# Where the residual stream is turned: the out projection's transposes and joins moved to the second stage's loads

## The chip, the cores and the metric

The kernel runs on one core of a Trainium2 chip. The metric is the device time of one launch in microseconds. It is 2405.47 us before the change (median of three runs, 2402.76 to 2409.40). One more execution was recorded by the hardware profiler; its own time is 2406.19 us.

## What is computed

The input x is 64 blocks of 64 channels by 1024 columns, which the kernel sees as 32 tiles of 128 tokens by H = 1024. Cut to what matters:

```python
x = x + attn(cond(x, itok_B_0_15, cond_weights), qkvw, qkvb, ow, ob)   # 32 heads of 32, softmax over 64
# second stage, cond2:
base   = x @ W.T
logits = x @ Wr.T + 5.0 * one_hot(language)        # 8 experts, the best 2, softmax of the two
lora   = sum over experts of ((x @ A_e.T) * gate_e) @ B_e
z      = base + 2.0 * lora
# feed-forward on z as bf16, each token scaled to 8 bits:
g, u   = quant(z * inv_gate) @ w_gate.T, quant(z * inv_up) @ w_up.T    # 512 wide
inter  = clip(silu(g) * u, -10, 10)
x      = x + quant(inter * inv_inter) @ w_down.T
```

`x` after the attention is called x1 here. It is needed twice: token by token, as the residual to which the last product is added, and turned (columns on the partitions, tokens along the free dimension), as the operand of the router and of `base`.

## The kernel before

The 32 tiles are taken in 16 pairs of 256 tokens. The attention works on blocks of 512 tokens and leaves its result, already turned, in DRAM. Then come two stages that run over the 16 pairs.

**The out projection** (`OutProjection`) multiplies a pair by `ow` with seven products (`Winograd`, in the order 1, 6, 7, 5, 2, 4, 3), each of 8 TensorE instructions of 128x512 in f32. Pairs 0 and 1 are woven into the end of the attention, pairs 2 to 15 run in the first loop of `second_stage`. Each product has a `rest` that adds into the tile x, which holds the input and the bias; after product 4 the first tile of the pair is complete, after product 3 the second. Each complete tile is then turned for the second stage (`turn`): 16-bit words are what a transposing DMA moves, so ScalarE copies each half of 512 columns into two planes, of low and of high halves of the words (`xh`), SP issues a transposing DMA from SBUF to SBUF (`xhT`), and some products later (`turned`) ScalarE joins the planes again into f32 words (`xTo`), which SP stores to `xT_d` in DRAM. The untouched tile is stored to the output, where the residual is kept. A pair takes four such turns.

**The second stage** is a software pipeline written out by hand: the loop body at the end of `second_stage` lists the steps of pairs p, p-1 and p-2, and each engine runs its own instructions in that order. For pair p, `load_x1` brings the pair's turned x1 in one DMA of 1 MB, a pair ahead; `router` multiplies it by the experts' matrices; `token_sums` makes the four sums that the seven products need, on VectorE; `route` chooses the experts on VectorE, with two small exponentials on ScalarE; `gates_transposed` turns the gates on TensorE (`ghp`) and ScalarE copies them to SBUF (`gT`); `lora` adds a product with gT to four of the seven products. What follows (`quant_a`, `quant_b`, `gate_or_up`, `glu`, `down`, `result`) belongs to the feed-forward. `quant_b` turns bf16 values by a transposing DMA issued by SP.

SP issues nearly all DMAs, in program order; one that has to wait for its data or its buffer holds up those behind it. Every DMA that SP issues also waits for the DMA that SP issued eight places before it, since eight semaphores are used in turn. Behind the out projection SP issues pair 1's load, and then the feed-forward's weights and rows of factors (`ig`, `iu`, `wg`, `wu`, `sg_w`, `su_w`, `ii`, `wd`, `sd_w`), 5.25 MB.

The last pair is done without the seven products (`undivided`), and its residual is read from the output (`x1_l`, `x1_ll`) and added by VectorE or GpSimd; the other pairs add by an accumulating DMA that GpSimd issues.

Of the kernel before, what the change touches and what calls it, by code (L numbers as in the profile page):

```python
# [11 lines left out]
F32 = mybir.dt.float32  # L12
# [8 lines left out]
P = 128  # L21
# [14 lines left out]
@with_exitstack  # L36
def adaln_attn_ffn(ctx: ExitStack, tc: tile.TileContext, a, out: bass.AP):
    nc = tc.nc
    x = a["x"]
    NB, C, H = x.shape  # L40
    NTOK = NB * C
    KC = H // P
    NT = NTOK // P
    BLK = 512
    PB = BLK // P
    NBLK = NTOK // BLK
    NCH = HEADS * HD // P
    HPC = P // HD

    x_t = x.rearrange("(i b) c t -> i (b c) t", b=2)  # L50
    out_t = out.rearrange("(i b) c t -> i (b c) t", b=2)

    const = ctx.enter_context(tc.tile_pool(name="const", bufs=1))
    dram = ctx.enter_context(tc.tile_pool(name="dram", bufs=1, space=bass.MemoryType.DRAM))

    ident = const.tile([P, P], F32, tag="ident", name="ident")
    make_identity(nc, ident)


    ctx_d = [  # L60
        dram.tile([P, NCH, 2 * P], F32, tag=f"ctx_d{p}", name=f"ctx_d{p}") for p in range(NT // 2)
    ]


    xT_d = [dram.tile([P, 2, KC, P], F32, tag=f"xT_d{p}", name=f"xT_d{p}") for p in range(NT // 2)]


    I = a["w_gate_t"].shape[1]
    srcs = {"wg": (a["w_gate_t"], KC, I), "wu": (a["w_up_t"], KC, I), "wd": (a["w_down_t"], I // P, H)}
    half = {  # L70
        nm: dram.tile([P, k, n], BF16, tag=nm + "_d", name=nm + "_d") for nm, (_, k, n) in srcs.items()
    }

    comb = {
        nm: dram.tile([P, 4, KC // 2, H // 2], F32, tag=nm + "_c", name=nm + "_c") for nm in ("wo", "wt")
    }
    any_i = const.tile([1, 1], I32, tag="any_i", name="any_i")
    with tc.manual_schedule(), ExitStack() as psum, ExitStack() as early:
        ps_g = psum.enter_context(tc.tile_pool(name="ps_g", bufs=4, space=PSUM, reuse_waits="tile"))
        st = early.enter_context(tc.tile_pool(name="halve", bufs=2))  # L80
        chores = halve_weights(tc, st, const, dram, srcs, half, any_i)
        chores = itertools.chain(chores, combine_quarters(tc, st, (("wo", a["ow"]), ("wt", a["w_t"])), comb))
        op = OutProjection(tc, a, x_t, out_t, ctx_d, xT_d, ps_g, comb, KC, H)
        attention(tc, a, x_t, ctx_d, ident, dram, ps_g, KC, PB, NBLK, NCH, HPC, H, C, chores, early, op)
        second_stage(tc, a, out_t, xT_d, ident, ps_g, KC, NT, H, C, half, comb, op)

    inexact = nc.values_load(any_i[0:1, 0:1], min_val=0, max_val=1)
    with tc.If(inexact != 0):
        feed_forward(tc, a, x_t, out_t, ctx_d, ident, KC, NT, PB, H, C, None)
# [1053 lines left out]
    B.update(T1=t1, T2=t2, T3=t3, T4=t4)  # L1143


def token_quarters(raw, KQ):
    return {f"B{h + 1}{t + 1}": raw[:, t, h * KQ:(h + 1) * KQ, :] for h in range(2) for t in range(2)}


def load_quarters(tc, pool, comb, nm, src, KQ, HH):  # L1150

    v = quarters(src)
# [14 lines left out]
class OutProjection:  # L1167

    def __init__(self, tc, a, x_t, out_t, ctx_d, xT_d, ps_g, comb, KC, H):
        self.tc, self.a, self.x_t, self.out_t, self.ctx_d, self.ps_g, self.comb = tc, a, x_t, out_t, ctx_d, ps_g, comb
        self.xT_d, self.turning = xT_d, []
        self.KC, self.H = KC, H
        self.NPAIR = len(ctx_d)
        self.stack = ExitStack()
        self.st = {}
# [38 lines left out]
        T = self.tp.tile([P, 4, KQ, P], F32, tag="T", name=f"To_{p}")  # L1216
        sums_of_tokens(self.tc.nc.vector, T, s["B"])

    def turn(self, p, t):

        nc, n = self.tc.nc, self.H // 2
        for f in range(2):
            h = self.hp.tile([P, 2, n], I16, tag="h", name=f"xh_{p}_{t}_{f}")
            nc.scalar.copy(h, planes(self.st[p]["x"][:, t, f * n:(f + 1) * n]))  # L1224
            hT = self.hp.tile([P, 2, n], I16, tag="hT", name=f"xhT_{p}_{t}_{f}")
            nc.sync.dma_start(
                hT.rearrange("p h (k q) -> p (h k) q", q=P), h.rearrange("p h n -> p (h n)"), transpose=True
            )
            self.turning.append((p, t, f, hT))

    def turned(self):
        nc, n, KQ = self.tc.nc, self.H // 2, self.KC // 2
        for p, t, f, hT in self.turning:
            xT = self.hp.tile([P, KQ, P], F32, tag="xT", name=f"xTo_{p}_{t}_{f}")
            nc.scalar.copy(planes(xT.rearrange("p k q -> p (k q)")), hT)  # L1235
            nc.sync.dma_start(self.xT_d[p][:, t, f * KQ:(f + 1) * KQ, :], xT)
        self.turning = []

    def pair(self, p):

# [4 lines left out]
        def one(i):  # L1245
# [8 lines left out]
            def rest():  # L1254
                x, ps = self.st[p]["x"], u.pop(("ps", i))
                if i in (6, 3):
                    self.turned()
                if i in (1, 6, 7):
                    u[i] = self.up.tile([P, HH], F32, tag=f"u{i}", name=f"ou{i}_{p}")
                    if i == 1:  # L1260
# [9 lines left out]
                if i == 5 and p + 1 < self.NPAIR:  # L1270
                    self.prepare(p + 1)
                if i in (4, 3):
                    self.turn(p, t)
                if i == 3:
                    for t in range(2):
                        nc.sync.dma_start(self.out_t[2 * p + t], x[:, t, :])
# [6 lines left out]
        return [one(i) for i in Winograd.ORDER]  # L1283


def second_stage(tc, a, out_t, xT_d, ident, ps_g, KC, NT, H, C, half, comb, op):


    nc = tc.nc
# [9 lines left out]
    with ExitStack() as ctx:  # L1299
# [2 lines left out]
        AT, loads_t = load_quarters(tc, wa, comb, "wt", a["w_t"], KQ, HH)  # L1302
        loads_t = iter(loads_t)
        ws = ctx.enter_context(tc.tile_pool(name="ws3", bufs=1, reuse_waits="tile", side="right"))
        xp1 = ctx.enter_context(tc.tile_pool(name="x3", bufs=2, reuse_waits="tile", side="right"))

        def load_row(name, src, n, pool=None):
            t = (pool or w).tile([P, n], F32, tag=name, name=name)
# [2 lines left out]

        st1 = {}

        def load_x1(p):
            s = st1[p] = {}
            s["xT"] = xp1.tile([P, 2, KC, P], F32, tag="x", name=f"x1T_{p}")
            nc.sync.dma_start(s["xT"], xT_d[p])

        awr = ws.tile([P, KC, ER + E], F32, tag="awr", name="awr")
        lang_i = ws.tile([P, NT], I32, tag="lang_i", name="lang_i")  # L1320
        bm = ws.tile([P, H], F32, tag="bm", name="bm")

        def first_loads():
            load_x1(0)
            nc.sync.dma_start(awr[:, :, 0:ER], a["a_t"].rearrange("(k p) n -> p k n", p=P))
            nc.sync.dma_start(awr[:, :, ER:ER + E], a["wr_t"].rearrange("(k p) n -> p k n", p=P))
            for r in range(2):
                nc.sync.dma_start(lang_i[r * C:(r + 1) * C, :], bcast_rows(a["lang"][r], C))
            nc.sync.dma_start(bm, a["b_t"].rearrange("e r o -> (e r) o"))


        for p in range(2, NPAIR):
# [5 lines left out]
                ld()  # L1338
            if p == NPAIR - 3:
                first_loads()  # L1340
        op.turned()
        op.stack.close()


# [3 lines left out]
        sm = ctx.enter_context(tc.tile_pool(name="sm3", bufs=2, reuse_waits="tile"))  # L1348

        st = st1  # L1350
        load_x1(1)
        ig = load_row("ig", a["inv_gate"], H)
        iu = load_row("iu", a["inv_up"], H)
        wt_b = {}
# [31 lines left out]

        def token_sums(p):
            s = st[p]
            s["B"] = token_quarters(s["xT"], KQ)
            T = p1p.tile([P, 4, KQ, P], F32, tag="T", name=f"T_{p}")  # L1390
            sums_of_tokens(nc.vector, T, s["B"])

        def router(p):
            s = st[p]
            pr = ps_h.tile([P, 2, ER + E], F32, tag="h", name=f"pr_{p}")
            for t in range(2):
                for k in range(KC):
                    nc.tensor.matmul(  # L1398
                        pr[:, t, :], s["xT"][:, t, k, :], awr[:, k, :],
                        start=(k == 0), stop=(k == KC - 1), skip_group_check=True,  # L1400
                    )
            s["pr"] = pr
# [76 lines left out]
        def undivided(p, t, n):  # L1479
# [5 lines left out]
            for h in range(2):  # L1485
                for k in range(KQ):
                    nc.tensor.matmul(
                        ps, s["xT"][:, t, h * KQ + k, :], AT[f"A{n + 1}{h + 1}"][:, k, :],
                        start=(h == 0 and k == 0), stop=(h == 1 and k == KQ - 1), skip_group_check=True,
                    )  # L1490

# [131 lines left out]
        def result(p, t, *adds):  # L1623
# [3 lines left out]
            for n in range(2):  # L1627
# [1 line left out]
                    y[:, hs[n]], s.pop(("pd", t, n)), si, sd_w[:, hs[n]], ALU.mult, ALU.mult  # L1629
                )  # L1630
                if adds:
                    adds[n % len(adds)].tensor_add(y[:, hs[n]], y[:, hs[n]], s["x", t][:, hs[n]])
                    nc.sync.dma_start(out_t[2 * p + t, :, hs[n]], y[:, hs[n]])
            if not adds:

# [8 lines left out]
        for p in range(NPAIR - 1):  # L1644
            q, r = p - 1, p - 2
            old, last = q >= 0, r >= 0
            do(p > 0, load_x1, p + 1)
            do(old, after, q, 3)
            do(last, scaled, r, 1, "u")
            do(last, glu, r, 1)  # L1650
# [9 lines left out]
            route(p)  # L1660
            after(p, 6)
            do(old, quant_b, q, 0, "u")
            base(p, 7)
            if p == NPAIR - 2:

# [18 lines left out]
            do(old, quant_b, q, 1, "u")  # L1684
            do(old, quant_a, q, 0, "i")
            base(p, 4)
            after(p, 4)
            do(old, gate_or_up, q, 1, "g")
            quant_a(p, 0, "g", (q, 0, "i") if old else None)
# [7 lines left out]


        p, q, r = NPAIR - 1, NPAIR - 2, NPAIR - 3
        st[q]["x", 1] = p1p.tile([P, H], F32, tag="xl", name="x1_l")  # L1700
        nc.sync.dma_start(st[q]["x", 1], out_t[2 * q + 1])
        xl = xp1.tile([P, 2, KC, P], F32, tag="x", name="x1_ll").rearrange("p t k n -> p t (k n)")
        for t in range(2):
            st[p]["x", t] = xl[:, t, :]
            nc.sync.dma_start(xl[:, t, :], out_t[2 * p + t])
        after(q, 3)
        scaled(r, 1, "u")
        glu(r, 1)
# [14 lines left out]
        quant_a(q, 1, "u", (q, 1, "g"))  # L1723
        completed(p, 0, 0)
        completed(p, 0, 1)
        rounded(p, 0, 0)
        rounded(p, 0, 1)
        result(r, 1)
# [104 lines left out]
```

## Time and profile before

| What | us |
|---|---|
| Median of three runs | 2405.47 |
| The profiled execution, its time | 2406.19 |
| The profiled execution, its span (first to last instruction) | 2404.4 |
| TensorE busy in the span | 2367.6 |
| VectorE, ScalarE, GpSimd busy | 1334.5, 936.2, 418.7 |
| Out projection, pairs 2 to 15 (1375 to 1712) | 24.0 a pair |
| Second stage, from 1712; a steady pair | 41.75 |

Times inside the profile are microseconds from the start of the span. In a timeline a line gives the start, the length, the engine, the line of the kernel, the operation with its output and inputs, how many instructions were merged, and in brackets how long the engine had been idle and what ended that. SPq is the instruction queue of SP, which issues DMAs: its length is the issue, not the transfer. A "transpose" on SP is a transposing DMA; a COPY of 128x1024 int16 on ScalarE is either a parting into planes (`xh<-xo`) or a join (`xTo<-xhT`).

The groups of the page that carry the turning, with busy time, mean of one in ns, and the idle time of the engine before them:

```profile
L1224 ACT COPY xh<-xo 128x1024 int16<-128x1024 int16 x64 | 64.4, 1041 | 142.8 <-DVE xo L1269 142.8
L1235 ACT COPY xTo<-xhT 128x1024 int16<-128x1024 int16 x64 | 84.7, 1337 | 58.4 <-DMA xhT<-xh 53.3
```

### The profile page before, as it was taken

Reading aid. Unit: us, or ns where it says so; the run is one execution under the profiler, and the core shown is the slowest. Engines: PE = TensorE matmul, PEld = TensorE weight load, DVE = VectorE, ACT = ScalarE, POOL = GpSimd, SP = SyncE. Lnnn points to the kernel's source line nnn. Section 1 sums busy time; section 2 is a strip of 40 time slices with the busy share of each in tenths; the row PEclk is TensorE's granted clock in tenths of the full one; section 3 lists DMA queues with packets and bytes.
Section 4 is the critical chain, followed back from the end, with each engine's and each line's share of the span. In section 5 each row is a group of like instructions: output and inputs, shape, how many; then the busy total and the mean of one; then the engine's idle time right before and its main releaser. Section 6 shows DMA issues by size and latency. Waiting matters only on the chain.

```text
span 2404.4 us, 41907 instructions
## 1 busy us (share of the span) xinstructions
PE 2367.6 (98%) x17066; PEld 1628.5 (68%) x17104; DVE 1334.5 (56%) x2584; ACT 936.2 (39%) x1220; POOL 418.7 (17%) x470
## 2 busy tenths in 40 slices
PE   8999999999999999999999999999999999999997
PEld 7888888888888888888888444444454545454452
DVE  3573474464543644633535533324377878777787
ACT  1344344343344443443434544343333333333333
POOL 4121112111122223220000333334100000000000
PEclk9999999999999999999999999999999999999999
DMA  7899799899899998997967788877733443444353
GB/s 229 217 240 248 190 228 241 221 232 220 208 232 274 212 255 230 242 237 179 207 188 196 213 257 258 275 218 248 239 77 75 90 79 83 84 86 82 70 119 76
DMA packets 612395, 453.84 MB, mean 189 GB/s; under 512 B 362465, under 2 KB 524258, under 8 KB 606690
## 3 DMA queue, kind: packets, MB, share of 16 engines
q1 hardware_dynamic: 581522, 393.91, 63.2%
q0 software_dynamic: 12240, 40.38, 7.9%
q10 hardware_dynamic: 18432, 16.79, 3.1%
q8 instruction: 137, 2.24, 0.4%
q14 instruction: 64, 0.52, 0.1%
HBM read 274.02 MB, written 91.23 MB: 152 GB/s over the span
## 4 chain that ended last, share of the span: by engine, by line
PE 92%; DMA 2%; DVE 1%; SPq 1%; issue 1%; ACT 0%; ACTq 0%; DVEq 0%
PE poa L1129 5%; PE poc L1129 5%; PE pod L1129 5%; PE psvc L530 4%; PE psva L530 4%; PE psvd L530 4%; PE pbc L1129 4%; PE pbd L1129 4%; PE pba L1129 4%; PE pskc L509 4%; PE pskd L509 4%; PE pska L509 4%; PE psqa L509 4%; PE psqd L509 4%; PE psqc L509 4%; PE pr L1398 2%
## 5 line engine op out<-in xcount | busy, mean ns | idle before, releaser
L582 ACT ACTIVATE prob<-prob 128x512 f32<-128x512 f32 x128 | 80.6, 629 | 346.7 <-DVE prob L578 338.6
L608 ACT COPY pT<-phT 128x1024 int16<-128x1024 int16 x128 | 165.4, 1339 | 25.4 <-DMA phT<-ph 21.4
L596 ACT COPY ph<-prob 128x1024 int16<-128x1024 int16 x128 | 133.5, 1043 | 63.1 <-DVE prob L590 38.4
L442 POOL COPY yB<-yhT 128x512 int16<-128x512 int16 (+1 forms) x84 | 75.8, 955 | 426.4 <-DMA yhT<-yh 426.4
L1636 POOL DMA_DIRECT2D out_dram<-y x29 | 25.2, 869 | 656.2 <-DVE y L1628 644.4
L577 DVE TENSOR_REDUCE mx<-s 128x8 f32<-128x512 f32 x128 | 87.4, 682 | 71.6 <-PE s L568 71.6
L1250 POOL TENSOR_TENSOR xo<-xo,ob 128x1024 f32<-128x1024 f32 x32 | 83.5, 2629 | 228.2 <-DVE prob L578 189.5
L509 PE MATMUL psqa<-yB,wq 128*128 128x256 f32 x512 | 121.1, 379 | 0.5 <-ACT psqp L479 0.5
L509 PE MATMUL pska<-yB,wk 128*128 128x256 f32 x512 | 120.9, 379 | 0.0
L1224 ACT COPY xh<-xo 128x1024 int16<-128x1024 int16 x64 | 64.4, 1041 | 142.8 <-DVE xo L1269 142.8
L530 PE MATMUL psva<-wv,yB 128*128 128x256 f32 x512 | 115.8, 379 | 0.0
L1129 PE MATMUL poa<-woA,cx 128*128 128x512 f32 x256 | 115.3, 593 | 0.0
L1129 PE MATMUL pba<-wtA,x1T 128*128 128x512 f32 x240 | 107.9, 592 | 0.0
L1235 ACT COPY xTo<-xhT 128x1024 int16<-128x1024 int16 x64 | 84.7, 1337 | 58.4 <-DMA xhT<-xh 53.3
L530 PEld LDWEIGHTS psva<-wv,yB 128*128 128x128 f32 x512 | 97.2, 190 | 14.0 <-issue 0.8
L509 PEld LDWEIGHTS psqa<-yB,wq 128*128 128x128 f32 x512 | 97.1, 190 | 14.0 <-ACT psqp L479 0.9
L509 PEld LDWEIGHTS pska<-yB,wk 128*128 128x128 f32 x512 | 97.3, 190 | 13.2
L633 ACT ACTIVATE co<-banks,bqkv 128x256 f32<-128x256 f32 x128 | 60.7, 474 | 109.3 <-PE banks L411 79.8
L1266 POOL TENSOR_TENSOR xo<-xo,ou 128x512 f32<-128x512 f32 x48 | 59.9, 1275 | 191.8 <-DVE ou L1263 191.8
L590 DVE TENSOR_TENSOR prob<-prob,den 128x512 f32<-128x512 f32 x128 | 89.4, 699 | 4.4
L578 DVE TENSOR_TENSOR prob<-s,mx 128x512 f32<-128x512 f32 x128 | 88.5, 691 | 4.5
L1129 PEld LDWEIGHTS poa<-woA,cx 128*128 128x128 f32 x256 | 48.5, 190 | 60.0 <-issue 59.5
(255 smaller groups left out, 4945.8 us busy)
## 6 DMA issues: line engine op xcount, KB each, us to landing
wv<-v_d SPq DMA_DIRECT2D x56, 512.0 KB
wq<-q_d SPq DMA_DIRECT2D x28, 1024.0 KB
wk<-k_d SPq DMA_DIRECT2D x28, 1024.0 KB
wq<-in_qkvw_dram SPq DMA_DIRECT2D x100, 256.0 KB
wk<-in_qkvw_dram SPq DMA_DIRECT2D x100, 256.0 KB
wv<-in_qkvw_dram SPq DMA_DIRECT2D x50, 512.0 KB
x<-in_x_dram SPq DMA_DIRECT2D x32, 512.0 KB
ctx_d<-co ACTq DMA_DIRECT2D x128, 128.0 KB
```

Of the source, the lines that this page charges most:

```text
L442: nc.gpsimd.tensor_copy(dst, src[:, :, :, halves[r] if hf else r])
L509: nc.tensor.matmul(ps[:, 0:HB], A[:, SLOT[A_OF[i]], k, :], B[B_OF[i]][:, k, :], start=first and k == 0, stop=k == KQ - 1, skip_group_check ...
L530: nc.tensor.matmul(ps[:, j * VC:(j + 1) * VC], B[B_OF[i]][:, k, j * P:(j + 1) * P], A[:, k, :], start=first and j == 0 and k == 0, stop=k ...
L577: nc.vector.tensor_reduce(mx, ps[:, :, n, :, :], AX.X, ALU.max)
L578: nc.vector.tensor_tensor(p.rearrange("p j h k -> p h j k"), ps[:, :, n, :, :], mx.unsqueeze(3).to_broadcast([P, HPC, 2, C]), ALU.subtract,)
L582: nc.scalar.activation(p, p, AF.Exp, scale=scale)
L590: nc.vector.tensor_tensor(p, p, den.unsqueeze(2).to_broadcast([P, n, C]), ALU.mult)
L596: nc.scalar.copy(h, planes(p.rearrange("p n k -> p (n k)")))
L608: nc.scalar.copy(planes(pT.rearrange("p a b q -> p (a b q)")), hT)
L1129: self.nc.tensor.matmul(ps, self.B[self.B_OF[i]][:, k, :], self.A[self.A_OF[i]][:, k, :], start=first and k == 0, stop=k == self.KQ - 1, s ...
L1235: nc.scalar.copy(planes(xT.rearrange("p k q -> p (k q)")), hT)
L1250: nc.gpsimd.tensor_add(s["x"][:, t, :], s["x"][:, t, :], self.ob)
```

## The change

The out projection parts each tile into planes as before, but both halves go into one tile `xh`, which SP stores as it is, 512 KB, to `x1_d` in DRAM. The transposes and the joins are taken out of the out projection. In the second stage the load of a pair becomes four transposing DMAs from DRAM (`turned_x1`), each for a quarter (half of the columns of one of the two tiles), and four joins on ScalarE (`joined_x1`). The turned pair is thus held in four tiles, of which there are seven buffers; the planes have two.

In the steady loop the first two transposes for pair p+1 are issued at the start of the loop body. Their joins stand behind `quant_b(q, 0, "u")`, followed by the other two transposes, whose joins stand between products 4 and 3. For pair 0 the first two transposes are issued behind pair 13 of the out projection and joined behind pair 14, and the other two issued behind pair 14 and joined behind pair 15. Pair 1's transposes are issued by the loop body of pair 0, which SP reaches after the weights; the load that stood ahead of the weights is gone. The last pair's residual is read in halves, its second tile later than before, into buffers of the turned pairs.

```diff
-    xT_d = [dram.tile([P, 2, KC, P], F32, tag=f"xT_d{p}", name=f"xT_d{p}") for p in range(NT // 2)]
+    x1_d = [dram.tile([2, P, 2, 2, H // 2], I16, tag=f"x1_d{p}", name=f"x1_d{p}") for p in range(NT // 2)]
...
-    def turn(self, p, t):
+    def part(self, p, t):
         nc, n = self.tc.nc, self.H // 2
+        h = self.hp.tile([P, 2, 2, n], I16, tag="h", name=f"xh_{p}_{t}")
         for f in range(2):
-            h = self.hp.tile([P, 2, n], I16, tag="h", name=f"xh_{p}_{t}_{f}")
-            nc.scalar.copy(h, planes(self.st[p]["x"][:, t, f * n:(f + 1) * n]))
-            hT = self.hp.tile([P, 2, n], I16, tag="hT", name=f"xhT_{p}_{t}_{f}")
-            nc.sync.dma_start(
-                hT.rearrange("p h (k q) -> p (h k) q", q=P), h.rearrange("p h n -> p (h n)"), transpose=True
-            )
-            self.turning.append((p, t, f, hT))
-    def turned(self):
-        nc, n, KQ = self.tc.nc, self.H // 2, self.KC // 2
-        for p, t, f, hT in self.turning:
-            xT = self.hp.tile([P, KQ, P], F32, tag="xT", name=f"xTo_{p}_{t}_{f}")
-            nc.scalar.copy(planes(xT.rearrange("p k q -> p (k q)")), hT)
-            nc.sync.dma_start(self.xT_d[p][:, t, f * KQ:(f + 1) * KQ, :], xT)
-        self.turning = []
+            nc.scalar.copy(h[:, f, :, :], planes(self.st[p]["x"][:, t, f * n:(f + 1) * n]))
+        self.parted.append((self.x1_d[p][t], h))
+    def stored(self):
+        for to, h in self.parted:
+            self.tc.nc.sync.dma_start(to, h)
+        self.parted = []
...
-        xp1 = ctx.enter_context(tc.tile_pool(name="x3", bufs=2, reuse_waits="tile", side="right"))
+        xp1 = ctx.enter_context(tc.tile_pool(name="x3", bufs=7, reuse_waits="tile", side="right"))
+        xh1 = ctx.enter_context(tc.tile_pool(name="xh3", bufs=2, reuse_waits="tile", side="right"))
...
-        def load_x1(p):
-            s = st1[p] = {}
-            s["xT"] = xp1.tile([P, 2, KC, P], F32, tag="x", name=f"x1T_{p}")
-            nc.sync.dma_start(s["xT"], xT_d[p])
+        QUARTERS = ((0, 1), (0, 0), (1, 0), (1, 1))
+        def turned_x1(p, *ns):
+            s = st1.setdefault(p, {"xT": {}})
+            for n in ns:
+                f, t = QUARTERS[n]
+                hT = s["hT", n] = xh1.tile([P, 2, HH], I16, tag="h", name=f"x1h_{p}_{n}")
+                nc.sync.dma_start(
+                    hT.rearrange("p h (k q) -> p (h k) q", q=P), x1_d[p][t].rearrange("q f h n -> q f (h n)")[:, f, :],
+                    transpose=True,
+                )
+        def joined_x1(p, *ns):
+            s = st1[p]
+            for n in ns:
+                f, t = QUARTERS[n]
+                x = s["xT"][t, f] = xp1.tile([P, KQ, P], F32, tag="x", name=f"x1T_{p}_{n}")
+                nc.scalar.copy(planes(x.rearrange("p k q -> p (k q)")), s.pop(("hT", n)))
...
         def first_loads():
-            load_x1(0)
+            turned_x1(0, 0, 1)
...
             if p == NPAIR - 3:
                 first_loads()
-        op.turned()
+            elif p > NPAIR - 3:
+                joined_x1(0, *((0, 1) if p == NPAIR - 2 else (2, 3)))
+                if p == NPAIR - 2:
+                    turned_x1(0, 2, 3)
+        op.stored()
...
-        load_x1(1)
         ig = load_row("ig", a["inv_gate"], H)
...
         for p in range(NPAIR - 1):
...
-            do(p > 0, load_x1, p + 1)
+            turned_x1(p + 1, 0, 1)
...
             do(old, quant_b, q, 0, "u")
+            joined_x1(p + 1, 0, 1)
+            turned_x1(p + 1, 2, 3)
             base(p, 7)
...
             base(p, 4)
+            joined_x1(p + 1, 2, 3)
             after(p, 4)
...
-        xl = xp1.tile([P, 2, KC, P], F32, tag="x", name="x1_ll").rearrange("p t k n -> p t (k n)")
-        for t in range(2):
-            st[p]["x", t] = xl[:, t, :]
-            nc.sync.dma_start(xl[:, t, :], out_t[2 * p + t])
+        def residual(t):
+            st[p]["x", t] = [
+                xp1.tile([P, KQ, P], F32, tag="x", name=f"x1_ll{t}_{n}").rearrange("p k q -> p (k q)") for n in range(2)
+            ]
+            for n in range(2):
+                nc.sync.dma_start(st[p]["x", t][n], out_t[2 * p + t, :, hs[n]])
+        residual(0)
...
         completed(p, 0, 1)
+        residual(1)
```

More of the change, by code (lines that the diff above doesn't have):

```diff
@@ L82, in adaln_attn_ffn @@
         chores = itertools.chain(chores, combine_quarters(tc, st, (("wo", a["ow"]), ("wt", a["w_t"])), comb))
-        op = OutProjection(tc, a, x_t, out_t, ctx_d, xT_d, ps_g, comb, KC, H)
+        op = OutProjection(tc, a, x_t, out_t, ctx_d, x1_d, ps_g, comb, KC, H)
         attention(tc, a, x_t, ctx_d, ident, dram, ps_g, KC, PB, NBLK, NCH, HPC, H, C, chores, early, op)
-        second_stage(tc, a, out_t, xT_d, ident, ps_g, KC, NT, H, C, half, comb, op)
+        second_stage(tc, a, out_t, x1_d, ident, ps_g, KC, NT, H, C, half, comb, op)
     inexact = nc.values_load(any_i[0:1, 0:1], min_val=0, max_val=1)
@@ L1143, in sums_of_tokens @@
     B.update(T1=t1, T2=t2, T3=t3, T4=t4)
-def token_quarters(raw, KQ):
-    return {f"B{h + 1}{t + 1}": raw[:, t, h * KQ:(h + 1) * KQ, :] for h in range(2) for t in range(2)}
 def load_quarters(tc, pool, comb, nm, src, KQ, HH):
@@ L1167, with __init__ @@
 class OutProjection:
-    def __init__(self, tc, a, x_t, out_t, ctx_d, xT_d, ps_g, comb, KC, H):
+    def __init__(self, tc, a, x_t, out_t, ctx_d, x1_d, ps_g, comb, KC, H):
         self.tc, self.a, self.x_t, self.out_t, self.ctx_d, self.ps_g, self.comb = tc, a, x_t, out_t, ctx_d, ps_g, comb
-        self.xT_d, self.turning = xT_d, []
+        self.x1_d, self.parted = x1_d, []
         self.KC, self.H = KC, H
@@ L1256, in rest @@
                 if i in (6, 3):
-                    self.turned()
+                    self.stored()
                 if i in (1, 6, 7):
@@ L1272, in rest @@
                 if i in (4, 3):
-                    self.turn(p, t)
+                    self.part(p, t)
                 if i == 3:
@@ L1283, in pair, with second_stage @@
         return [one(i) for i in Winograd.ORDER]
-def second_stage(tc, a, out_t, xT_d, ident, ps_g, KC, NT, H, C, half, comb, op):
+def second_stage(tc, a, out_t, x1_d, ident, ps_g, KC, NT, H, C, half, comb, op):
     nc = tc.nc
@@ L1388, in token_sums @@
             s = st[p]
-            s["B"] = token_quarters(s["xT"], KQ)
+            s["B"] = {f"B{f + 1}{t + 1}": x for (t, f), x in s["xT"].items()}
             T = p1p.tile([P, 4, KQ, P], F32, tag="T", name=f"T_{p}")
@@ L1398, in router @@
                     nc.tensor.matmul(
-                        pr[:, t, :], s["xT"][:, t, k, :], awr[:, k, :],
+                        pr[:, t, :], s["xT"][t, k // KQ][:, k % KQ, :], awr[:, k, :],
                         start=(k == 0), stop=(k == KC - 1), skip_group_check=True,
@@ L1487, in undivided @@
                     nc.tensor.matmul(
-                        ps, s["xT"][:, t, h * KQ + k, :], AT[f"A{n + 1}{h + 1}"][:, k, :],
+                        ps, s["xT"][t, h][:, k, :], AT[f"A{n + 1}{h + 1}"][:, k, :],
                         start=(h == 0 and k == 0), stop=(h == 1 and k == KQ - 1), skip_group_check=True,
@@ L1631, in result @@
                 if adds:
-                    adds[n % len(adds)].tensor_add(y[:, hs[n]], y[:, hs[n]], s["x", t][:, hs[n]])
+                    adds[n % len(adds)].tensor_add(y[:, hs[n]], y[:, hs[n]], s["x", t][n])
                     nc.sync.dma_start(out_t[2 * p + t, :, hs[n]], y[:, hs[n]])
@@ L1699, in second_stage @@
         p, q, r = NPAIR - 1, NPAIR - 2, NPAIR - 3
-        st[q]["x", 1] = p1p.tile([P, H], F32, tag="xl", name="x1_l")
-        nc.sync.dma_start(st[q]["x", 1], out_t[2 * q + 1])
-        xl = xp1.tile([P, 2, KC, P], F32, tag="x", name="x1_ll").rearrange("p t k n -> p t (k n)")
-        for t in range(2):
-            st[p]["x", t] = xl[:, t, :]
-            nc.sync.dma_start(xl[:, t, :], out_t[2 * p + t])
+        xl = p1p.tile([P, H], F32, tag="xl", name="x1_l")
+        st[q]["x", 1] = [xl[:, hs[n]] for n in range(2)]
+        nc.sync.dma_start(xl, out_t[2 * q + 1])
+        def residual(t):
[5 more added lines that the diff above has]
+        residual(0)
         after(q, 3)
```

## The prediction

> **What bounds the kernel now.** I read the page's busy table first, then stretches of time, then the timelines of PE, ACT and SP where the second stage begins.
>
> ```profile
> PE 2367.6 (98%) x17066; PEld 1628.5 (68%) x17104; DVE 1334.5 (56%) x2584; ACT 936.2 (39%) x1220; POOL 418.7 (17%) x470
> ```
>
> TensorE is idle for only 36.8 us of 2404.4, so work moved between other engines gains only where PE waits. The view of stretches (length; busy us of PE, PEld, DVE, ACT, POOL; granted clock; DMA share; GB/s) shows the out projection, the DMA burst behind it, and one steady pair of the second stage:
>
> ```profile
> 1330.00:1712.00 382.00, 382.00 (x1140) 170.05 (x1139) 136.51 (x172) 166.04 (x161) 143.88 (x82) 1.00 0.77 238
> 1720.00:1728.00 8.00, 8.00 (x20) 3.60 (x19) 4.38 (x21) 3.33 (x5) 0.00 (x0) 1.00 0.91 321
> 1728.00:1742.00 14.00, 13.54 (x34) 5.93 (x33) 2.73 (x4) 0.96 (x2) 0.00 (x0) 1.00 0.96 380
> 1742.00:1746.00 4.00, 4.00 (x23) 2.80 (x22) 1.59 (x5) 2.21 (x2) 0.00 (x0) 1.00 0.04 15
> 1866.08:1907.83 41.75, 41.64 (x146) 20.88 (x148) 33.30 (x72) 14.30 (x19) 1.72 (x2) 1.00 0.41 82
> ```
>
> In the out projection PE is busy 382.00 of 382.00 us: the turning taken away from there costs no PE time today. The burst is the second stage's weights, and the DMA engines are full until about 1742. At the seam of the stages, PE, then ACT, then SP:
>
> ```profile
> 1711.99 3.87 PE L1398 MATMUL pr<-awr,x1T 128*128 128x136 f32 x32
> 1729.43 0.38 PE L1458 MATMUL ghp<-ident,gh 128*128 128x128 f32 x2
> 1730.28 1.12 PE L1463 MATMUL pbd<-bm,gT 128*128 128x512 f32 x2 [0.46 <-ACT gT L1460]
> ```
>
> ```profile
> 1714.71 1.98 ACT L1224 COPY xh<-xo 128x1024 int16<-128x1024 int16 x2
> 1718.57 2.74 ACT L1235 COPY xTo<-xhT 128x1024 int16<-128x1024 int16 x2 [1.88 <-DMA xhT<-xh]
> 1725.34 0.19 ACT L1437 ACTIVATE g<-d 128x2 f32<-128x2 f32 x1
> 1729.85 0.37 ACT L1460 COPY gT<-ghp 128x256 f32<-128x256 f32 x1 [4.33 <-PE ghp L1458]
> ```
>
> ```profile
> 1715.77 2.58 SPq L1226 DMA_TRANSPOSE xhT<-xh  x2
> 1718.45 1.01 SPq L1276 DMA_DIRECT2D out_dram<-xo  x2
> 1721.70 0.46 SPq L1317 DMA_DIRECT2D x1T<-xT_d  x1
> 1730.94 0.33 SPq L1309 DMA_DIRECT2D sd_w<-in_s_wdown_dram  x1
> ```
>
> PE goes from the last out projection product straight into the first router, because pair 0's turned tile landed long before; ACT's last joins (to 1721.3) are on nobody's path. PE's only wait here is 0.46 us for gT.
>
> **The change, part by part.**
>
> *Removed from the out projection:* per pair 4 joins on ACT of 1.337 us (5.3), 4 transposes on SP of 1.24 us (5.0), and 4 stores of 256 KB become 2 of 512 KB. With PE at 382.00 of 382.00 this is worth 0 us; the cover was PE's own 24.0 us per pair.
>
> *Added in a steady pair:* 4 joins, 5.3 us, to ACT's 14.30 of 41.75 us, and 4 transposes (5.0 us of SP) in place of one load of 0.57. The rows that must hide them:
>
> ```profile
> 2012.48 0.37 ACT L1460 COPY gT<-ghp 128x256 f32<-128x256 f32 x1 [7.42 <-PE ghp L1458]
> 2029.15 1.15 ACT L1562 ACTIVATE q_g<-q_g,rs_g 128x1024 f32<-128x1024 f32 x1 [3.87 <-DVE rs_g L1561]
> ```
>
> The first two joins stand ahead of gT, in 7.42 us of idle time; the other two ahead of q_g, in 3.87 us. Each couple takes 2.67, which fits with 4.7 and 1.2 us to spare. On SP the first couple of transposes goes out right after 1990.16, and the next SP instruction ran at 2000.83; the second couple waits for the first joins (2007.7, as it has two buffers) and holds back qT_g, due at 2017.91. So 0 us, as long as a transpose has landed before its join. If a cover went, each microsecond would be paid in about 14 pairs.
>
> *The end:* two of the last residual loads now wait on SP for PE's second product of the last pair (2348.0), ahead of qT_u, which ran at 2352.18. Two issues of 0.43 us fit: 0.
>
> *The seam, first wait.* Pair 0's last two joins now stand on ACT behind the last out projection tile's two copies. DVE finishes that tile at 1712.96 (its add began 1712.27), the copies end at 1715.0 (1.98 us), the joins at 1716.4 and 1717.7. The router consumes a quarter in 0.93 us and needs a joined one second and fourth: it waits from 1712.9 to 1716.4 and ends at 1719.2 instead of 1715.7. That is +3.5 us.
>
> *The seam, second wait.* Pair 1's transposes now stand on SP behind all the weights, where its load stood ahead of them, and its first two joins stand on ACT ahead of gT of pair 0. When do those transposes land? Before, the burst ended near 1742. The two output stores now go out at 1713.0 instead of 1718.45, as no transposes are ahead of them: -5.4. The load x1T, 1.05 MB at the 321 GB/s of its stretch, is gone: -3.3. Two transposes from DRAM come in. No row shows one; the nearest is the transpose from SBUF, 0.26 MB, which kept the DMA engines busy for 1.31 us (1758.4 to 1759.7). Below, it is a plain load at 380 GB/s, 0.7 us; above, half of the pair of xhT transposes whose SP issue took 4.72 us in traffic, 2.4 us. I take 1.3, the nearest kind: +2.6. So they land near 1736; the second join ends at 1737.4, gT at 1737.8, and the product that needs gT starts at 1737.9 instead of 1730.3. That is +7.6, and it contains the 3.5 (PE arrives at 1733.7 and idles about 4 more). Queued behind gT on PE is all else, so nothing later wins it back: PE is full up to 2370.
>
> [...]
>
> *The clock.* After a thin stretch of PE the trace shows it fall:
>
> ```profile
> 2388.00:2392.00 4.00, 1.39 (x10) 0.49 (x9) 3.79 (x8) 1.94 (x3) 1.25 (x2) 1.00 0.00 0
> 2392.00:2394.00 2.00, 2.00 (x7) 0.80 (x8) 1.97 (x4) 0.00 (x0) 2.00 (x2) 0.68 1.01 113
> ```
>
> With 1.39 us of work in 4 us the granted clock went to 0.68, and 8 products of the down projection took 2.87 us instead of 1.90: 0.97 lost. After gaps below 2 us it stayed 1.00. Two gaps of 3.5 and 4 us lie nearer to the thin stretch: I take +1.0 (ends: 0, and 2.0 if both pay; a loss after the first gap hides under the second).
>
> [...]
>
> **Sum.** 7.6 + 1.0 = +8.6 us on the profiled execution: its span becomes 2413.0, its time 2414.8 (2406.19 before). Around the median 2405.47 that is 2414.1. The forecast's own range: +5 (burst drained at 430 GB/s, the rate seen at 1738) to +14 (7.1 MB from 1714.3 at 321 GB/s, transposes of 2.4 us each: landing 1741, gT 1742.8, +12.5, clock 1.5).
>
> **Rivals.**
> *A, only the router waits.* If the transposes get past the weights on the DMA engines, pair 1's joins are done before gT is due, and only 3.5 us remain: 2409.0, no change by my bound. Against it: all of these go through one queue (q1), and sd_w, issued last, came with the end of the burst. For it: the page gives no landing times for single DMAs of this queue. It decides if the second landing is before 1731.
> *B, transposes from DRAM are slow in every pair.* Between a couple's issue (1991.4) and the next transpose that PE needs soon (qT_i at 2000.83) lie 10 us: from 5 us each, four times the row, they push qT_i back. At 8 us each it is 6 us a pair, 14 pairs: 2414 + 84 = 2498. Against it: the loads of 4 to 8 us, partly rows of 512 B, ran at 379 to 416 GB/s. [...]
> *C, faster.* Lighter ACT and SP queues in the first two out projection pairs remove the 0.82 us that PE waits for pT at 1311.65, and both seam waits vanish because ACT is ahead: 2404.7. Against it: the first transpose removed was issued at 1350, after that wait, and nothing else idles PE there.
>
> **How the numbers follow.** Forecast 0.74, A 0.12, B 0.09, C 0.05. Likeliest: 2414. A measurement here tells 0.3%, 7.2 us, from no change. Of the forecast's 0.74 some 0.14 lies below +7.2; with A and 0.02 of C, same is 0.28. Slower: 0.60 + 0.09 = 0.69; faster 0.03. The range 2408 to 2422 takes in A and the forecast's ends with 1.5 to 2 us for the scatter of medians; B and C are left out.
>
> **What would show it.** Right: one PE gap of 3 to 4 us inside the first router, released by ACT's join; one of 3 to 6 us ahead of the product with gT, with ACT waiting for the transpose's landing; a clock below 1.00 after one; 41.75 us per pair unchanged; 24.0 in the out projection. Wrong: no wait at gT (A), pairs longer than 41.75 (B), or a third gap, at the second router or in the tail.

## The result, and the profile after

The changed kernel takes 2413.27 us (median of 17 runs, 2408.50 to 2421.93), the kernel before, in 17 runs on the same chip, 2401.78 us (2398.86 to 2409.40). The medians differ by 11.5 us. The ratio over all runs is 1.0040, with a 95% interval from 1.0031 to 1.0049, which is 9.6 us (7.4 to 11.8). The profiled execution of the changed kernel took 2421.93 us, the slowest of its 17, with a span of 2420.0 us. The page's busy table, and from the list of all groups the two that now carry the turning:

```profile
PE 2376.8 (98%) x17104; PEld 1631.5 (67%) x17104; DVE 1376.6 (57%) x2584; ACT 933.6 (39%) x1220; POOL 422.6 (17%) x470
```

```profile
L1322 ACT COPY x1T<-x1h 128x1024 int16<-128x1024 int16 x64 | 80.8, 1327 | 8.9 <-DMA x1h<-x_d 8.9
L1220 ACT COPY xh<-xo 128x1024 int16<-128x1024 int16 x64 | 63.9, 1043 | 264.4 <-DVE xo L1258 239.9 <-issue 15.6 <-ACT xh L1220 8.0
```

The 64 joins take what they took before (1327 ns each against 1337). They wait for their transposes 8.9 us in the whole kernel; before, the joins waited 53.3 us for DMAs, at a place where no one needed them. So one wait is left. The stretches show where it lies (length; busy us of PE, PEld, DVE, ACT, POOL; granted clock; DMA share; GB/s). First the out projection and a steady pair:

```profile
1330.00:1716.69 386.69, 386.69 (x1275) 172.76 (x1273) 179.71 (x176) 91.93 (x103) 148.54 (x82) 1.00 0.57 198
1881.52:1923.27 41.75, 41.75 (x148) 20.87 (x147) 33.30 (x72) 19.16 (x23) 1.72 (x2) 1.00 0.50 82
```

PE is as full in the out projection as before, and a pair of the second stage lasts 41.75 us as before, with ScalarE at 19.16 us instead of 14.30. Between the two lies the seam; I call so the stretch from the first router's first product to the second router's first. In the stretches its middle and its end read:

```profile
1717.80:1721.00 3.20, 0.00 (x0) 0.00 (x0) 1.54 (x6) 3.20 (x4) 0.00 (x0) 1.00 0.81 332
1721.00:1725.60 4.60, 4.60 (x25) 4.60 (x26) 1.90 (x3) 1.15 (x1) 0.00 (x0) 0.63 0.82 305
...
1739.70:1743.00 3.30, 0.00 (x0) 0.00 (x0) 0.00 (x0) 2.74 (x3) 0.00 (x0) 0.86 0.33 65
1743.00:1745.00 2.00, 1.98 (x3) 0.95 (x4) 0.00 (x0) 0.00 (x0) 0.00 (x0) 0.50 0.89 162
1745.00:1750.30 5.30, 5.30 (x9) 2.15 (x8) 0.69 (x1) 0.00 (x0) 0.00 (x0) 0.63 0.20 36
1750.30:1759.77 9.47, 9.47 (x23) 4.18 (x22) 3.46 (x5) 3.42 (x4) 0.00 (x0) 1.00 0.00 0
```

Two stretches with PE at 0.00, and behind each a granted clock of 0.50 to 0.63. The timelines of PE, ACT and SP name what ended them:

```profile
1716.69 1.09 PE L1406 MATMUL pr<-awr,x1T 128*128 128x136 f32 x8
1721.00 4.72 PE L1406 MATMUL pr<-awr,x1T 128*128 128x136 f32 x24 [3.22 <-ACT x1T L1322]
...
1739.29 0.38 PE L1466 MATMUL ghp<-ident,gh 128*128 128x128 f32 x2
1743.02 2.08 PE L1471 MATMUL pbd<-bm,gT 128*128 128x512 f32 x2 [3.35 <-ACT gT L1468]
1744.89 5.60 PE L1129 MATMUL pba<-wtA,x1T 128*128 128x512 f32 x8
```

```profile
1717.73 1.99 ACT L1220 COPY xh<-xo 128x1024 int16<-128x1024 int16 x2 [2.43 <-DVE xo L1258]
1719.63 2.52 ACT L1322 COPY x1T<-x1h 128x1024 int16<-128x1024 int16 x2
...
1740.23 2.51 ACT L1322 COPY x1T<-x1h 128x1024 int16<-128x1024 int16 x2 [8.86 <-DMA x1h<-x_d]
1742.62 0.35 ACT L1468 COPY gT<-ghp 128x256 f32<-128x256 f32 x1
```

```profile
1725.22 0.33 SPq L1299 DMA_DIRECT2D sd_w<-in_s_wdown_dram  x1
1726.51 17.66 SPq L1312 DMA_TRANSPOSE x1h<-x_d  x4
```

The router uses up its joined quarter, then waits for two joins that stand behind the last tile's two copies. Later ScalarE sits 8.86 us idle in front of pair 1's joins, whose transposes were issued behind the last of the weights (`sd_w`); gT, whose input was there at 1739.7, has to wait behind them, and PE behind gT. The eight products of 5.60 us took 3.60 before: that is the clock.

The seam lasted 32.13 us before (1711.99 to 1744.12) and lasts 43.08 after (1716.69 to 1759.77), 10.95 more. In parts: the product with gT starts 26.33 us after the router instead of 18.29, so 8.04 for the waits, and from there to the second router it takes 16.75 instead of 13.84, so 2.91 for the clock behind the second gap. The 8.04 contain the first gap and what the clock loses behind it: PE cannot go on before gT is there, however early it arrives (shown below by the early joins). The rest of the span behind the second router is 660.23 us against 660.28. What is left of the 15.6 us between the two spans, 4.7 us, lies ahead of the first router.

### The profile page after: what moved, and what is told of

Its sections match the earlier page's. It is cut to its first block, busy times and chain, and to the rows that moved or that the text cites. A ratio compares the mean times of both kernels' runs of the same rounds, so it can differ in the third digit from the quotient of the medians.

```text
span 2420.0 us, 41797 instructions
## 1 busy us (share of the span) xinstructions
PE 2376.8 (98%) x17104; PEld 1631.5 (67%) x17104; DVE 1376.6 (57%) x2584; ACT 933.6 (39%) x1220; POOL 422.6 (17%) x470
## 4 chain that ended last, share of the span: by engine, by line
PE 70%; DMA 1%; DVE 1%; ACT 0%; issue 0%; SPq 0%; POOL 0%; ACTq 0%; POOLq 0%; DVEq 0%
PE poa L1129 5%; PE pod L1129 5%; PE poc L1129 5%; PE pba L1129 4%; PE pbc L1129 4%; PE pbd L1129 4%; PE pr L1406 2%; PE pskc L509 2%; PE pskd L509 2%; PE psvc L530 2%; PE pska L509 2%; PE psva L530 2%; PE psvd L530 2%; PE pob L1129 2%; PE pu L1597 2%; PE psqa L509 2%
## 5 line engine op out<-in xcount | busy, mean ns | idle before, releaser
L588 DVE TENSOR_REDUCE den<-prob 128x8 f32<-128x512 f32 x128 | 86.4, 675 | 0.0
```

The lines of the kernel that those rows point to most:

```text
L588: nc.vector.tensor_reduce(den, p, AX.X, ALU.add)
```

## The experiments

All times of a row are from its profile, but for the medians. "gT" is the start of the product with gT, counted from the start of the first router.

| Kernel | median us (runs) | ratio to before, 95% interval | router starts | gT | seam |
|---|---|---|---|---|---|
| before | 2401.78 (17) | | 1711.99 | 18.29 | 32.13 |
| before, again | 2408.39 (1) | | 1714.40 | 18.29 | 32.12 |
| after | 2413.27 (17) | 1.0040, 1.0031 to 1.0049 | 1716.69 | 26.33 | 43.08 |
| after, again | 2416.55 (6) | 1.0053, 1.0039 to 1.0068 | 1709.95 | 26.56 | 42.09 |
| transposes ahead of the weights | 2408.74 (11) | 1.0021, 1.0010 to 1.0033 | 1711.25 | 23.44 | 37.28 |
| last joins early | 2414.37 (5) | 1.0038, 1.0025 to 1.0051 | 1709.01 | 26.12 | 42.22 |
| both | 2403.58 (11) | 0.9997, 0.9988 to 1.0006 | 1708.71 | 18.28 | 32.12 |
| joins behind gT | 2407.88 (12) | 1.0016, 1.0005 to 1.0027 | 1708.67 | 23.44 | 37.28 |
| gaps filled | 2412.22 (12) | 1.0034, 1.0022 to 1.0047 | 1709.55 | 26.31 | 40.04 |
| 2 MB more in front | 2421.26 (4) | 1.0069, 1.0054 to 1.0084 | 1710.34 | 31.67 | 47.55 |

The kernel before, beside which each ratio is taken, had a median of 2403.71 us in 29 runs with the first four experiments and of 2404.30 us in 17 runs with the others, so between these groups the ratios can be compared, not the medians. A load or a transpose "lands" when its last data is there.

**Transposes ahead of the weights.** Pair 1's first two transposes go back to where its load stood.

```diff
+        turned_x1(1, 0, 1)
         ig = load_row("ig", a["inv_gate"], H)
...
-            turned_x1(p + 1, 0, 1)
+            do(p > 0, turned_x1, p + 1, 0, 1)
```

> Pair 1's first two transposes are issued ahead of the weights instead of behind them. The seam (from the start of the first router to the start of the second one) took 32.1 us before the change and 43.1 us after it. Theory (two waits of PE, each in an engine's or a queue's order, and a clock that falls after each): the wait for gT goes, and with it the clock loss behind it; the wait of the first router stays (3.2 us), and its clock loss (1.9 us), which lay hidden in front of the second wait, is now paid: seam 37 us, time 5 to 6 us below the changed kernel, some 2407. Rival 1 (the transposes land late wherever they are issued, since they share the DMA engines with the weights): the wait for gT stays, seam 41 to 43. Rival 2 (only the gT wait costs): seam 32 to 34.

The seam is 37.28 us, 5.15 above before, and the excess over before fell from 11.5 to 5.0 us. PE's timeline:

```profile
1711.25 1.09 PE L1407 MATMUL pr<-awr,x1T 128*128 128x136 f32 x8
1715.56 4.72 PE L1407 MATMUL pr<-awr,x1T 128*128 128x136 f32 x24 [3.22 <-ACT x1T L1322]
...
1734.69 1.13 PE L1472 MATMUL pbd<-bm,gT 128*128 128x512 f32 x2 [0.46 <-ACT gT L1469]
1735.65 3.60 PE L1129 MATMUL pba<-wtA,x1T 128*128 128x512 f32 x8
```

The wait for gT is the 0.46 us of the kernel before, and the products behind it are at full speed. What is left is the router. PE is idle for 3.22 us, and the 24 products behind that take 4.55 us to the start of the next one (1720.11), where 2.78 is the time at full clock (3.87 for all 32 less 1.09 for the first eight): 1.77 for the clock, granted at 0.62 there. The remaining 0.16 of the 5.15 is the modelled end of the first eight products, from which the idle time is counted. In the changed kernel this was paid as well, but under the second wait.

**Last joins early.** The opposite half: pair 0's last two joins go ahead of the last tile's copies.

```diff
                 product()
+                if (p, n) == (NPAIR - 1, 6):
+                    joined_x1(0, 2, 3)
                 rest()
...
-            elif p > NPAIR - 3:
-                joined_x1(0, *((0, 1) if p == NPAIR - 2 else (2, 3)))
-                if p == NPAIR - 2:
-                    turned_x1(0, 2, 3)
+            elif p == NPAIR - 2:
+                joined_x1(0, 0, 1)
+                turned_x1(0, 2, 3)
```

> Pair 0's last two joins are put ahead of ScalarE's copies of the last out projection tile, so that the first router need not wait for them. Theory (the first wait is contained in the second): PE's wait of 3.2 us in the first router is gone, but gT still waits for the landing of pair 1's transposes: the wait there grows from 3.3 us to about 8 us, the seam stays at 42 to 44 us and the time within 1 us of the changed kernel. Rival (the two waits add up): the seam falls by 3 to 5 us, to 38 to 40.

The router runs through, and nothing is won: 2414.37 us, seam 42.22. PE's timeline:

```profile
1709.01 3.87 PE L1407 MATMUL pr<-awr,x1T 128*128 128x136 f32 x32
...
1735.13 2.08 PE L1472 MATMUL pbd<-bm,gT 128*128 128x512 f32 x2 [8.30 <-ACT gT L1469]
1737.00 4.95 PE L1129 MATMUL pba<-wtA,x1T 128*128 128x512 f32 x8
```

PE arrives earlier and waits 8.30 us instead of 3.35 for the same landing: the product with gT starts 26.12 us after the router, as in the changed kernel (26.33). The waits don't add up; the first is contained in the second.

**Both edits together.**

> Both edits together: pair 1's first two transposes ahead of the weights, pair 0's last two joins ahead of the last tile's copies. Theory: both waits and all of the clock loss are gone, the seam is 32 to 33 us again, and the time is that of the kernel before within 2 us, although the turning in the second stage (joins, transposes from DRAM) stays as the change has it. Rival 1 (the moved turning itself costs in the steady pairs or upstream): the seam is 32 to 33 but the time stays 4 us or more above the kernel before. Rival 2 (the landing is late in any order): seam 40 or more.

The time is that of the kernel before (0.9997, 0.9988 to 1.0006), with every transpose from DRAM and every join still in the second stage. Its stretches, cut at the product with gT:

```profile
1708.71:1726.99 18.28, 17.82 (x67) 9.88 (x65) 8.81 (x32) 8.00 (x10) 0.00 (x0) 1.00 0.96 321
1726.99:1740.83 13.84, 13.84 (x33) 6.19 (x33) 4.15 (x6) 3.54 (x4) 0.00 (x0) 1.00 0.69 185
```

18.28 and 13.84 us, against 18.29 and 13.84 before, clock 1.00. The whole loss of the change is these two places of order; the moved work itself costs nothing that these runs can tell and, off a bound PE, shows no gain either (the interval is -2.9 to +1.4 us). No version beat the kernel before.

**Joins behind gT.** The transposes stay behind the weights; in pair 0 alone ScalarE takes gT first.

```diff
-            joined_x1(p + 1, 0, 1)
-            turned_x1(p + 1, 2, 3)
+            if p > 0:
+                joined_x1(p + 1, 0, 1)
+                turned_x1(p + 1, 2, 3)
...
             gates_transposed(p)
+            if p == 0:
+                joined_x1(1, 0, 1)
+                turned_x1(1, 2, 3)
```

> The transposes stay behind the weights on SP; in pair 0 alone ScalarE takes gT first and pair 1's first two joins (with the issue of the other two transposes) behind it. Theory (gT is late only since it stands behind the joins in ScalarE's order): the wait for gT falls below 1 us although the transposes land as late as in the changed kernel, near 1735 to 1740; the router's wait and its clock loss remain: seam 37 us, as with the transposes ahead of the weights, time some 2407. Rival (gT is late for its own inputs, or PE needs the joined tile soon after): the wait for gT stays at 3 us or turns up ahead of the second router, seam 40 to 43.

The seam is 37.28 us, as with the transposes ahead. ScalarE's timeline:

```profile
1731.68 0.37 ACT L1468 COPY gT<-ghp 128x256 f32<-128x256 f32 x1 [8.34 <-PE ghp L1466]
1732.76 2.54 ACT L1322 COPY x1T<-x1h 128x1024 int16<-128x1024 int16 x2 [0.70 <-DMA x1h<-x_d]
```

The transposes land as late as before: the first join starts at 1732.76, 24.1 us after the router (23.5 in the changed kernel). But gT no longer stands behind it, and the second router, which needs pair 1, is not late. So the landing alone hurts nobody; it hurt through ScalarE's order.

**Gaps filled.** PE gets products that nothing reads, where it waits.

```diff
+        def filled(name, n):
+            ps = ps_h.tile([P, HH], F32, tag="h", name=f"fill_{name}")
+            for j in range(n):
+                nc.tensor.matmul(
+                    ps, st[0]["xT"][0, 0][:, j % KQ, :], AT["A11"][:, j % KQ, :], start=(j == 0), stop=(j == n - 1)
+                )
...
+                    if p == 0 and (t, k) == (0, KQ):
+                        filled("r", 4)
...
+            if p == 0:
+                filled("g", 6)
```

> The changed kernel with products that nothing reads in both gaps of PE, 8 instructions (3.4 us) after the router's first quarter and 12 (5.2 us) after the gates' transpose, into a spare buffer of PSUM. They end about when the wait that they lie in ends. Theory (2.9 us of the seam are a granted clock that falls after an idle stretch of PE): the clock stays at 1.00, the two products with gT take 1.1 us and the eight behind them 3.6 (2.1 and 5.6 in the changed kernel), and the seam is 40.0 to 40.6 us, 2.5 to 3 us below the changed kernel's 43.1. Rival (these products are slow from the DMA traffic or from the landing itself, not from idling): the clock is low there again, and the seam is 43 us or more.

The stretches of the two fills and of what follows each:

```profile
1709.55:1716.76 7.21, 7.21 (x42) 5.15 (x41) 4.09 (x11) 4.43 (x4) 0.00 (x0) 1.00 0.88 316
...
1730.71:1735.86 5.15, 5.15 (x14) 2.23 (x13) 0.00 (x0) 2.76 (x3) 0.00 (x0) 1.00 0.54 103
1735.86:1749.59 13.73, 13.73 (x33) 6.08 (x33) 4.14 (x6) 3.43 (x4) 0.00 (x0) 1.00 0.21 37
```

The clock stays at 1.00, the 16.75 and 15.53 us that the two profiles of the changed kernel have from the product with gT to the second router become 13.73, and the seam is 40.04 us, though gT is as late as ever (26.31). So the last 2 to 3 us of the change's loss come from PE's idling, not from the traffic around it.

**Two megabytes more in front of the transposes.**

```diff
+    for n in range(2):
+        half["copy", n] = dram.tile([P, I // P, H], BF16, tag=f"copy{n}", name=f"copy{n}")
...
         sd_w = load_row("sd_w", a["s_wdown"], H)
+        for n in range(2):
+            nc.sync.dma_start(half["copy", n], half["wd"])
```

> The changed kernel with two more loads that nothing reads, copies of 1 MB from DRAM to DRAM, behind the last of the weights and ahead of pair 1's transposes. Theory (the second wait is as long as it takes the DMA engines to empty what stands ahead of the transposes): 2.1 MB more at the 310 to 373 GB/s of the burst put the landing off by 5.6 to 6.8 us, and the seam goes from 43.1 to 48.5 to 50 us. Rival (the wait is set by the transposes' own duration or by SP's order, not by the bytes in front): 43 to 44 us.

The product with gT starts 31.67 us after the router, 5.1 to 5.3 later than in the two profiles of the changed kernel, and the seam is 47.55 us: the theory's direction, but half a microsecond under its range for the landing and one under it for the seam. 2.10 MB in 5.1 to 5.3 us are 393 to 411 GB/s, more than the 373 I had put in. Why was not tried: the stretches behind that figure also held stores and transposes, and these copies go from DRAM to DRAM. The clock cost 2.04 here instead of 2.91. SP's timeline:

```profile
1720.59 2.98 SPq L1376 DMA_DIRECT2D copy<-wd_d  x2
1725.59 17.55 SPq L1315 DMA_TRANSPOSE x1h<-x_d  x4
```

The bytes in front act through SP here. It issues the first transpose 15.25 us after the router instead of 9.82 and 9.97, and the DMA eight places ahead, for which it waits, is now the load of `wu` (1 MB) and was that of `iu` (512 KB, 0.9 us of waiting in the profile of the changed kernel); from issue to landing it takes 13.6 us, in the changed kernel 13.7 and 13.8. In the changed kernel the DMA engines are full from the issue to the landing (DMA share 0.99); in this run their share is 0.69 over the 8.69 us of PE's second gap, 5.89 of which lie ahead of the landing. So the wait grows with the bytes in front, but this run does not part a longer queue from a later issue.

**The two kernels again.** These ask where the 4.7 us ahead of the router come from.

> The changed kernel as it is, for a second profile. Of the 15.6 us between the two profiled spans 10.95 lie in the seam (32.1 before, 43.1 after) and 4.7 ahead of it: the first router starts at 1712.0 before and at 1716.7 after. Theory (the 4.7 us are the scatter of the unchanged attention: that profiled run was the slowest of its 17, and in the four experiments, whose code ahead of the seam is that of the changed kernel, the router starts at 1708.7 to 1711.3): the router starts between 1707 and 1714, the seam is 43 us again. Rival (the lighter queues of the first pairs cost time in the attention): the router starts at 1716 or later again.

> The kernel before as it is, for a second profile. Theory: the seam is 32.1 us again, and the first router starts within 4 us of 1712.0, by the scatter of the attention. Rival (the start is fixed for each kernel): 1712.0 within 0.5 us.

The changed kernel's router starts at 1709.95 this time, that of the kernel before at 1714.40: the sign is reversed. Over the eight profiles with the changed out projection it starts between 1708.67 and 1716.69. The first product of the out projection, ahead of which the change touches nothing, starts at 1322.50 before and 1327.22 after, and from there to the router it is 389.49 and 389.47 us. So the 4.7 us lie in the attention and are its scatter, not the change. The seam of the kernel before is the same to 0.01 us; that of the changed kernel is 42.09, below the 43 expected, and the difference is the clock: 1.69 us behind the second gap instead of 2.91, while gT came 0.23 later. PE's timeline of the changed kernel this time:

```profile
1714.26 5.80 PE L1406 MATMUL pr<-awr,x1T 128*128 128x136 f32 x24 [3.22 <-ACT x1T L1322]
...
1736.51 1.63 PE L1471 MATMUL pbd<-bm,gT 128*128 128x512 f32 x2 [2.49 <-ACT gT L1468]
```

Behind the second router 660.08 us follow before and 660.76 after.

## Why the prediction was right, step by step

**What costs nothing.** Held throughout. PE stayed full in the out projection, a pair stayed at 41.75 us, the tail and all behind the second router stayed within 0.7 us, and with the seam mended the time is that of before. In the steady pairs no join waited for its transpose.

**The first wait.** Forecast 3.5 us of idling, inside the second wait; 3.22 were measured, and the early joins showed the inclusion. By itself it costs 5.15, since the clock then falls too. For the same reason PE reaches the second gap later than forecast: it was to idle about 4 us there, and idled 3.35 and 2.49.

**The second wait.** Forecast 7.6 us; 8.04 and 8.27 were measured. The mechanism (transposes behind the weights on SP, joins ahead of gT on ScalarE) was shown from both sides: each order undone alone removes the wait. The landing of both transposes was put at 24.0 us after the router, and the end of the second join at 25.4; the first join began 23.5 and 23.8 after it, and the second ended at 26.05 and 26.28. My unknown price, 1.3 us of DMA time for one transpose from DRAM, can now be estimated. In a steady pair of the changed kernel the view of DMA use over 2007.4 to 2012.4 us, which holds nothing but transposes (a couple from DRAM and part of one from SBUF), reads:

```profile
## 3 DMA queue, kind: packets, MB, share of 16 engines
q1 hardware_dynamic: 2878, 0.71, 83.3%
```

0.71 MB in 83.3% of 5.0 us is 4.17 us, so by this estimate 0.262 MB, the size of a quarter, takes about 1.5 us, 170 GB/s while busy; that is a mean over both kinds.

**The clock.** This is the term that was mis-sized: 1.0 us forecast, 2.91 and 1.69 measured behind the second gap (2.26 and 2.04 in two experiments). I had put the gaps near the tail's thin stretch, which lost 0.97, but kept between it and no loss.

**The sum.** 8.6 us were forecast; the seam grew by 10.95 and 9.97 in the two profiles, and the whole time by 11.5 us by the medians or 9.6 by the ratio. That 2414 came out so close to 2413.27 owes something to chance: the three runs that I started from had a median of 2405.47, and 17 runs gave 2401.78. By the medians, a base 3.7 us too high and a sum 2.9 us too low met.

**The rivals.** A (only the router waits) fails with the wait at gT; it is what two of the experiments built, at 1.0021 and 1.0016. B (slow transposes in every pair) fails with the 41.75 us: a transpose lands 4.8 us after its issue in the median, and no join but the seam's ever waited. C (both waits vanish, something gained upstream) fails in the seam.

## What to carry to other kernels

When work moves off an engine that is not the bound, price the places where its order changes, not its length: here 64 joins and 64 transposes cost nothing in the steady state, and two positions in two queues cost all of it. Look first at the seam between two stages, where a load that used to be ahead of a burst is now behind it, and ask what stands behind the instruction that waits for it. Two waits in a row on one chain don't add up; undo both, since undoing one shows half or nothing. And look for what a gap on a full TensorE costs on top in its clock: here 1.69 to 2.91 us behind gaps of 2.49 to 8.69 us.

## What the runs showed of the hardware

**The clock's loss does not follow the gap's length.** Behind the second gap: 2.49 us of idling lost 1.69, 3.35 lost 2.91, 8.30 lost 2.26, 8.69 lost 2.04. Behind the first one: always 3.22 us of idling, and 1.77 or 1.78 lost in four profiles, 2.82 in the fifth (the changed kernel again, where the 24 products take 5.60 us to the start of the next one, at a granted clock of 0.50). In the stretches that end within 8 us behind a second gap (the two profiles of the changed kernel and the early joins) the granted clock is 0.50 to 0.73; with the gaps filled it stayed at 1.00. What sets the loss between 1.69 and 2.91 us was not shown.

**VectorE beside GpSimd.** In the out projection VectorE's busy time rose from 136.51 to 179.71 us (the second window is 4.7 us longer and holds 176 instructions instead of 172), though the change gives it nothing to do. VectorE's and GpSimd's timelines in one pair of the changed kernel:

```profile
1514.99 1.00 DVE L1139 TENSOR_TENSOR To<-cx 128x512 f32<-128x512 f32 x1
1516.02 2.72 DVE L1140 TENSOR_TENSOR To<-cx,To 128x512 f32<-128x512 f32 x1
1518.66 2.83 DVE L1141 TENSOR_TENSOR To<-cx 128x512 f32<-128x512 f32 x1
1521.41 0.68 DVE L1142 TENSOR_TENSOR To<-cx,To 128x512 f32<-128x512 f32 x1
```

```profile
1515.40 5.55 POOL L1239 TENSOR_TENSOR xo<-xo,ob 128x1024 f32<-128x1024 f32 x2
```

Two sums stretch, to 2.72 and 2.83 us, over GpSimd's two additions of 2.8 us each, and the sum behind them takes 0.68 us. In the kernel before, in the pair around 1513 us, one sum (L1142, 2.83 us) met the additions and the three others took 0.69. What stretches the sums was not tried by itself, and it costs nothing here, since PE was full all the while.
